# Finishing and sending batch 14's output by chunk instead of by bank, with one feature sum moved to VectorE and two steps moved ahead of a turn in batch 1's period

## The chip, the cores and the metric

The kernel runs on one core of one Trainium2 chip. The metric is the device time of one execution in microseconds; the figure for a kernel is the median of its runs. Besides the plain runs one execution was taken with a hardware profile, and every time with a place in the program comes from that one.

## The reference

The program computes a two-direction graph attention for 16 batches of 512 nodes with 512 features. The 20 first nodes of a batch are its keys and values; the adjacency carries 11 labels for each pair. Cut to what matters:

```python
row_zero = exp_v.sum(-1) == 0
q_exp = jnp.where(row_zero[..., None], 0.0, q[:, None, :])
self_feat = jnp.concatenate([exp_v, q_exp], -1) @ W_self.T + b_self
output = self_feat
for d in range(2):
    A = adj_f if d == 0 else jnp.swapaxes(adj_f, 1, 2)
    A = A[:, :, :20, :]
    aff = einsum(qh, kh) / sqrt(32)          # 16 heads of 32
    aff = where(A.sum(-1) > 0, aff, -9e15) + (A @ w_bias + b_bias)
    w = softmax(aff)
    output += einsum(w, kv, Wout[d]) + bout[d]
return exp_v + relu(output)
```

## The kernel before, in words

Everything is float32. After a set-up of some 90 us that multiplies the weights into keys and values, the main loop (`for b in range(B - 1)`, L1065) runs one period for each batch 0 to 14, and batch 15 is written out by hand behind it (L1263 to L1349). No scheduler reorders anything: each engine works through its instructions in the order of the code, and a semaphore holds an instruction until what it needs is there.

TensorE has three kinds of work in a period. `self_product` (L641, matmuls on L661) makes the features of batch b+1 in seven products of half size, where sums of operands replace an eighth product. `score_product` (L404, matmuls on L397) makes the scores of batch b in seven products in the same way, from feature blocks, key blocks and their sums. `attend` (L559, matmuls on L568) multiplies the softmax weights of batch b-1 with its values.

The scores of a batch lie in four blocks (c, l): c is the key half, l the node half. Products 1 and 6 accumulate in one PSUM tile `ps_a`. Between products its intermediate sums are read out: `taken` (L494, ScalarE) reads it after 1 and again after 7, and `lowered` (L501, VectorE, L502) reads it after 6 and again after 4. Product 7 accumulates into the same `ps_a`, so it may only start once `lowered` has read what stands there after 6. For each block follow `joined_with` (L506, VectorE), `weigh` (L515, VectorE: row maximum L522 and subtraction L523), `expo` (L525, ScalarE), `total` (L529, VectorE: row sum L531 and reciprocal L532), `normal` (L534, GpSimd multiplication L536) and `turn` (L540, VectorE transposition L544).

The operand sums are `feat_sum` n = 1 to 4 (L372; sum 1 on L377, the others on L384) and `key_sum`, on GpSimd unless an engine is given; sum 2 is made from sum 1, and sum 3 feeds score product 7. For batch b+1 `self_join` (L682, VectorE), `self_lift` (L684, VectorE, two instructions on L686) and `self_copy` (L679, ScalarE) empty the feature products; `mask_count` (L329) and `mask_sum` (L335) reduce the labels on VectorE. Loads are issued on SyncE's queue, some held until a named step is done, so that they go out in turn: `load_x` of the batch after next has its first quarter behind the lift, its second behind the label count; `load_cq` (two small loads of key biases) stands behind a turn.

Before `attend(b-1)` ScalarE seeds the four PSUM banks with the features (`seed_out`, L554, instructions on L555): banks 2 and 3 early, banks 0 and 1 late in the period, behind `expo(b, 1, 0)` and a `self_copy` on ScalarE's queue.

Output: `outt[b]` holds four chunks of 128 features by 512 nodes, and each chunk is one DMA of 128x512 float32 (262,144 bytes, `store`, L615). A PSUM bank a of `outsum` holds half the nodes (in turns of 32) of two chunks: banks 0 and 1 together make chunks 0 and 1, banks 2 and 3 make chunks 2 and 3. `finish` (L581, VectorE, L585) or `relieve` and `residual` (L590 on ScalarE, L597 on GpSimd, L600) do relu and the addition of x for one bank, hence for half of two chunks. `end` (L602) does the same for one chunk out of both banks: on VectorE with two instructions of 256 elements (L610), or on ScalarE (L612) and then GpSimd (L613). Before the change only batch 15, the last one, uses `end`; batch 14 (called `o`) goes by bank, chunks 2 and 3 being sent after the second `residual`, chunks 0 and 1 after the second `finish`.

Of the kernel before, what the change touches and what calls it, by code (L numbers as in the profile page):

```python
# [9 lines left out]
AF = mybir.ActivationFunctionType  # L10
# [8 lines left out]
def gat_kernel(  # L19
# [20 lines left out]
    nc = tc.nc  # L40
    B, F, N = xT.shape
# [10 lines left out]
    R = P // HL  # L52
# [11 lines left out]
    ps_s = ctx.enter_context(tc.tile_pool(name="ps_s", bufs=2, space=PSUM))  # L64
# [28 lines left out]
    sums, parts, done, cleared = {}, {}, {}, []  # L93
# [3 lines left out]
    def behind(one, other):  # L97

        if other is not None:
            info = mybir.DependencyInfo(mybir.DependencyClass.Sync, mybir.DependencyReason.DATA)  # L100
            tc.add_manual_dep(one.ins, other.ins.name, info, reason="loads in turn")
# [23 lines left out]
    def load_cq(b, ins=None):  # L125
        cqs[b] = load.tile([P, 2, HL, S], F32, tag="cq", name=f"cq{b}")
        for p in range(2):
            behind(nc.sync.dma_start(
                cqs[b][bass.ts(p, P // 2)].rearrange("p c h m -> p (c h m)"),
                cq_d[b : b + 1, bass.ts(p, H // 2)].rearrange("b h d m -> b (h d m)").partition_broadcast(P // 2),  # L130
            ), ins if p == 0 else None)
# [197 lines left out]
    def mask_count(b, h):  # L329
        a = adjs[b, h]  # L330
        cond = msk.tile([P, 2 * S], F32, tag="cond", name=f"cond{b}_{h}")
        done["count"] = nc.vector.tensor_reduce(cond, a.rearrange("p t (m l) -> p (t m) l", l=L), AX.X, ALU.add)  # L332
        nc.gpsimd.tensor_scalar(prods[b, h][:, :, L], cond, 0.0, NEG, ALU.is_le, ALU.mult)  # L333
# [20 lines left out]
    def feat_block(b, f, l):  # L354
        return sfs[b][:, 2 * f : 2 * f + 2, bass.ts(l, N // 2)]
# [16 lines left out]
    def feat_sum(b, n, engine=nc.gpsimd):  # L372

        if n < 4:
            fsums[b, n] = xsum.tile([P, 2, N // 2], F32, tag=f"f{n}", name=f"f{b}_{n}")
        if n == 1:
            engine.tensor_add(fsums[b, 1], feat_block(b, 0, 1), feat_block(b, 1, 1))  # L377
            return
        to, one, two = {
            2: lambda: (fsums[b, 2], fsums[b, 1], feat_block(b, 0, 0)),  # L380
            3: lambda: (fsums[b, 3], feat_block(b, 0, 0), feat_block(b, 0, 1)),
            4: lambda: (fsums[b, 2], feat_block(b, 1, 0), fsums[b, 2]),
        }[n]()
        done["fsum"] = engine.tensor_sub(to, one, two)  # L384

    def pair(name, n):
        return ps_s.tile([P, HL, N // 2], F32, tag=f"s{n % 2}", name=name, bufs=1)
# [141 lines left out]
    def total(b, c, l):  # L529
        sm = smalls[b, c, l] = soft.tile([P, per], F32, tag="sm", name=f"sm{b}_{c}{l}")  # L530
        nc.vector.tensor_reduce(sm, heads(weighs[b, c, l]), AX.X, ALU.add)  # L531
        done["sum"] = nc.vector.reciprocal(sm, sm)  # L532

    def normal(b, c, l):  # L534
        f = heads(weighs[b, c, l])
        done["normal"] = nc.gpsimd.tensor_mul(  # L536
            f, f, smalls.pop((b, c, l)).unsqueeze(2).to_broadcast([P, per, NG])
        )

    def turn(b, c, l):  # L540

        if b not in wts:
            wts[b] = work.tile([P, 2, 2, W], F32, tag="wt", name=f"wt{b}")
        done["turn"] = nc.vector.transpose(wts[b][:, c, l], weighs.pop((b, c, l)).rearrange("p g w -> p (g w)"))  # L544

    def new_outs(b, homes=None):
        homes = homes or ((accs, "f0"), (accs, "f1"), (accs, "c"))
        tiles = [
            pool.tile([P, 1 + (tag[0] != "f"), 512], F32, tag=tag, name=f"ps_o{b}_{tag}", bufs=1) for pool, tag in homes
        ]  # L550
        outsum.setdefault(b, []).extend(t[:, u] for t in tiles for u in range(t.shape[1]))
        return tiles
# [24 lines left out]
    def spread_out(t, a):  # L577

        return t[:, a // 2 * 2 : a // 2 * 2 + 2].rearrange("p c (n u r) -> p c u n r", u=2, r=R)[:, :, a % 2]

    def finish(b, a):  # L581

        if b not in outt:
            outt[b] = work.tile([P, C, N], F32, tag="o", name=f"o{b}", bufs=1)
        done["out", a] = nc.vector.scalar_tensor_tensor(  # L585
            spread_out(outt[b], a), outsum[b][a].rearrange("p (c n r) -> p c n r", c=2, r=R), 0.0,
            spread_out(xs[b], a), ALU.max, ALU.add,
        )

    def relieve(b, a):  # L590

        if b not in outt:
            outt[b] = work.tile([P, C, N], F32, tag="o", name=f"o{b}", bufs=1)
        to = spread_out(outt[b], a)
        nc.scalar.activation(to, outsum[b][a].rearrange("p (c n r) -> p c n r", c=2, r=R), AF.Relu)

    def residual(b, a):  # L597

        to = spread_out(outt[b], a)
        nc.gpsimd.tensor_add(to, to, spread_out(xs[b], a))  # L600

    def end(b, p, c, engine, us=slice(0, 2)):  # L602

        to, of = (
            t[:, 2 * p + c].rearrange("p (n u r) -> p u n r", u=2, r=R)[:, us] for t in (outt[b], xs[b])
        )
        ps = ends[p][:, us, bass.ts(c, N // 2)].rearrange("p u (n r) -> p u n r", r=R)
        if engine is nc.vector:
            for u in range(2):
                nc.vector.scalar_tensor_tensor(to[:, u], ps[:, u], 0.0, of[:, u], ALU.max, ALU.add)  # L610
        else:
            nc.scalar.activation(to, ps, AF.Relu)  # L612
            engine.tensor_add(to, to, of)  # L613

    def store(b, cs, ins=None):  # L615
        for c in cs:
            behind(nc.sync.dma_start(out[b, bass.ts(c, P)], outt[b][:, c]), ins)
# [63 lines left out]
    def self_join(b, f, l):  # L681
        done["joined"] = nc.vector.tensor_add(block(b, f, l), feed(b, 1), block(b, f, l))  # L682
# [10 lines left out]
    with tc.tile_pool(name="setup", bufs=1) as sp, tc.tile_pool(name="ps_acc", bufs=4, space=PSUM) as acc["pool"]:  # L693
# [18 lines left out]
        with tc.tile_pool(name="setup_k", bufs=1) as sk:  # L712
# [77 lines left out]
            ps = ps_s.tile([P, 2, 512], F32, tag="s1", name="ps_q", bufs=1)  # L790
# [11 lines left out]
            for fc in range(C):  # L802
                qp = sk.tile([P, B, NG], F32, tag="qp", name=f"qp{fc}", bufs=4)
                engine = nc.gpsimd if fc else nc.vector
# [49 lines left out]
        with tc.tile_pool(name="setup_g", bufs=3) as sg:  # L854
# [138 lines left out]
            for n, runs in enumerate(bursts):  # L993
# [14 lines left out]
                if rest:  # L1008
                    for kind in "mm" if n else ():
                        f, args = steps[kind].pop(0)  # L1010
# [3 lines left out]
                for kind in plan[n - first] if n - first < len(plan) else ():  # L1014
                    f, args = steps[kind].pop(0)
# [38 lines left out]
    accs = ctx.enter_context(tc.tile_pool(name="ps_loop", bufs=1, space=PSUM))  # L1054
# [5 lines left out]
    with tc.manual_schedule():  # L1060
# [4 lines left out]
        for b in range(B - 1):  # L1065
            one, two, more, further = b > 0, b > 1, b + 1 < B, b + 2 < B

            def at(yes, f, *args):
                if yes:
                    f(*args)  # L1070
# [8 lines left out]
                    load_xn(2, 1)  # L1079
            if b == 1:  # L1080
                self_join(1, 0, 1)
                feat_sum(1, 1)
                feat_sum(1, 2)
                total(0, 1, 0)
                normal(0, 1, 0)
                turn(0, 1, 1)
# [59 lines left out]
                spill(1)  # L1146
            lowered(b, 1, 0)
            at(more, load_keys, b + 1, range(3, 4), done["lowered"])
            at(one, turn, b - 1, 0, 1)
            at(one and more, load_cq, b + 1, done.get("turn"))  # L1150
            if more:
                self_product(b + 1, 6)
                self_lift(b + 1)
                at(further, load_x, b + 2, range(1), done["lift"])
                mask_count(b + 1, 0)
            at(further, load_x, b + 2, range(1, 2), done["count"])
            turn(b, 0, 0)
            at(further, load_x, b + 2, range(2, 3), done["turn"])
# [104 lines left out]
        b = B - 1  # L1263
        o = b - 1
# [15 lines left out]
        weigh_plain(b, 0, 0)  # L1280
        turn(o, 0, 1)
        seed_block(b, 0, 1, [pair("ps_l", 1)])
        new_outs(o, ((accs, "c"),))
        outt[o] = load.tile([P, C, N], F32, tag="x0", name=f"o{o}", bufs=1)
        seed_out(o, 0)
        seed_out(o, 1)
# [6 lines left out]
        store(b - 2, range(2, 4))  # L1293
        plain_scores(b, 0, 1)
        weigh_plain(b, 1, 0)
        new_outs(o, ((ps_s, "s0"),))
        seed_out(o, 2)
        seed_out(o, 3)
        seed_block(b, 1, 1, [accs.tile([P, 2, N // 2], F32, tag=f"f{i}", name=f"ps_e{i}") for i in range(2)])
# [3 lines left out]
        normal(b, 1, 0)  # L1303
        plain_scores(b, 1, 1, range(2))
        weigh_plain(b, 0, 1)
        ends = new_outs(b, ((ps_s, "s1"),))
        turn(b, 1, 0)
        for q in (3, 2):
            relieve(o, q)
        seed_out(b, 0)  # L1310
        seed_out(b, 1)
        total(b, 0, 1)
        normal(b, 0, 1)
        residual(o, 3)
        finish(o, 0)
        ends += new_outs(b, ((ps_s, "s0"),))
        seed_out(b, 3)
        plain_scores(b, 1, 1, range(2, 4))
        weigh_plain(b, 1, 1, 0)
# [1 line left out]
        turn(b, 0, 1)  # L1321
        total_part(b, 1, 1, 0)
        normal_part(b, 1, 1, 0, nc.gpsimd)
        residual(o, 2)
        store(o, range(2, 4))
        weigh_plain(b, 1, 1, 1)
        turn_part(b, 1, 1, 0)
        attend(b, ((0, 0, 2), (1, 0, 1)))
        total_part(b, 1, 1, 1)
        normal_part(b, 1, 1, 1, nc.vector)  # L1330
        turn_part(b, 1, 1, 1)
        finish(o, 1)
        store(o, range(2))
        spare = const.tile([P, C, WD], F32, tag="g", name=f"o{b}", bufs=1).rearrange("p c w -> p (c w)")
        outt[b] = spare[:, : C * N].rearrange("p (c n) -> p c n", c=C)

        def send(queue, c):
            queue.dma_start(out[b, bass.ts(c, P)], outt[b][:, c])

        end(b, 1, 0, nc.gpsimd)  # L1340
        send(nc.sync, 2)
        end(b, 0, 0, nc.gpsimd, slice(1, 2))
        attend(b, ((1, 1, 2),))
        end(b, 0, 0, nc.gpsimd, slice(0, 1))
        end(b, 1, 1, nc.vector)
        send(nc.sync, 3)
        end(b, 0, 1, nc.vector)
# [48 lines left out]
```

## Time and profile before

| | |
|---|---|
| median of 3 runs | 551.27 us (551.25 to 552.41) |
| the profiled execution, its own time | 551.43 us |
| its span, first to last instruction | 549.7 us |
| granted TensorE clock, mean | 0.997 |
| TensorE busy | 539.7 us (98% of the span) |
| VectorE busy | 480.2 us (87%) |
| ScalarE, GpSimd busy | 404.2 us (74%), 435.8 us (79%) |

The span is 1.7 us shorter than the execution's own time. A timeline row gives the start in us from the span's start, how long the row lasts, the engine and line, the output and inputs by the program's names with their shapes, how many instructions the row merges, and in brackets how long the engine stood idle just before and what ended that. PE is a matmul, PEld a weight load on the same engine, SPq the issue of a DMA by SyncE's queue. A row of the windows view gives the stretch, its length, the busy time of each engine, the granted clock, the share of the DMA engines and GB/s.

### The profile page before, as it was taken

The page shows a single profiled execution, that of the slowest core. Times are in us where ns is not written, and L with a number is a line of the kernel's source. Part 1 is how long each engine was busy: PE and PEld are TensorE (multiplying, and loading weights), DVE is VectorE, ACT ScalarE, POOL GpSimd, SP SyncE. Part 2 cuts the span into 40 slices and gives each one's busy share as a digit, 9 for nine tenths or more (in the row PEclk, how much of TensorE's full clock was granted, in tenths as well). Part 3 has the DMA queues.
Part 4 walks back from the last instruction along what each step waited for, and adds up shares of the span by engine and source line. Part 5 has one row for each costly group of instructions (what it writes and reads, how often), then busy time and mean ns, then how long its engine had stood idle before and what let it go on. Part 6 is the DMA issues. An engine that isn't in the chain of part 4 may idle for free.

```text
span 549.7 us, 19621 instructions
## 1 busy us (share of the span) xinstructions
PE 539.7 (98%) x7908; PEld 423.6 (77%) x7908; DVE 480.2 (87%) x708; ACT 404.2 (74%) x999; POOL 435.8 (79%) x420
## 2 busy tenths in 40 slices
PE   9999999999999999999999999999999999999994
PEld 6544368889788878787888878888878787888783
DVE  1776678888999999999999999999999999999995
ACT  1225436797897979888888888888878787877662
POOL 2637896779979797979798888888888979797565
PEclk9999999999999999999999999999999999999998
DMA  8999999978786878778776858676777677735034
GB/s 299 376 394 369 306 372 339 316 211 261 210 255 190 230 222 226 222 221 236 211 223 191 242 178 231 197 235 186 233 201 221 205 219 197 216 117 172 2 117 154
DMA packets 100530, 126.45 MB, mean 230 GB/s; under 512 B 19592, under 2 KB 68678, under 8 KB 98392
## 3 DMA queue, kind: packets, MB, share of 16 engines
q1 hardware_dynamic: 98696, 121.93, 71.1%
q0 software_dynamic: 1168, 2.23, 1.7%
q8 instruction: 62, 1.02, 0.8%
q10 hardware_dynamic: 576, 1.05, 0.5%
q14 instruction: 28, 0.23, 0.1%
HBM read 86.23 MB, written 40.24 MB: 230 GB/s over the span
## 4 chain that ended last, share of the span: by engine, by line
PE 91%; DVE 3%; DMA 3%; POOL 1%; ACT 1%; issue 1%; SPq 0%; DVEq 0%; POOLq 0%
PE ps_f L661 31%; PE ps_a L397 23%; PE ps_c L397 11%; PE ps_d L397 6%; PE ps_o_f L568 5%; PE ps_k L829 3%; PE ps_v L887 2%; PE ps_o_c L568 2%; DMA ws_q<-in_wsT 1%; PE ps_a L284 1%; DMA g_d<-st 1%; PE ps_l L397 1%; PE ps_c L284 1%; PE ps_e L397 0%; PE ps_d L284 0%
## 5 line engine op out<-in xcount | busy, mean ns | idle before, releaser
L327 ACT ACTIVATE prod<-adj,wb_sb 128x80 f32<-128x80 int32 x330 | 116.0, 430 | 0.0
L536 POOL TENSOR_TENSOR w<-w,sm 128x640 f32<-128x640 f32 x63 | 80.2, 1274 | 33.4 <-DVE sm L532 32.3
L661 PE MATMUL ps_f<-t,ws_s 128*64 128x246 f32 x720 | 80.0, 370 | 0.0
L661 PEld LDWEIGHTS ps_f<-t,ws_s 128*64 128x64 f32 x720 | 51.7, 136 | 18.9
L527 ACT ACTIVATE w<-w 128x640 f32<-128x640 f32 x60 | 43.8, 730 | 18.6 <-DVE w L523 18.6
L544 DVE STREAM_TRANSPOSE wt<-w 128x640 f32<-128x640 f32 x63 | 52.5, 834 | 1.3 <-POOL w L536 1.2
L661 PE MATMUL ps_f<-x,ws_v 128*64 128x246 f32 x480 | 52.4, 371 | 0.0
L531 DVE TENSOR_REDUCE sm<-w 128x32 f32<-128x640 f32 x63 | 51.1, 811 | 1.1 <-ACT w L527 0.9
L522 DVE TENSOR_REDUCE ps_d<-w 128x32 f32<-128x640 f32 x59 | 48.7, 826 | 1.8 <-ACT ps_d L431 0.2
L523 DVE TENSOR_TENSOR w<-w,ps_d 128x640 f32<-128x640 f32 x59 | 48.4, 821 | 2.0
L661 PEld LDWEIGHTS ps_f<-x,ws_v 128*64 128x64 f32 x480 | 34.7, 137 | 13.0
L370 POOL TENSOR_TENSOR k<-g,k 128x608 f32<-128x608 f32 x30 | 44.7, 1490 | 0.0
L397 PEld LDWEIGHTS ps_a<-g,sf 128*64 128x64 f32 x544 | 34.2, 137 | 5.9 <-issue 5.8
L397 PE MATMUL ps_a<-g,sf 128*64 128x152 f32 x544 | 38.6, 295 | 0.0
L338 DVE TENSOR_REDUCE add<-prod 128x80 f32<-128x960 f32 x32 | 36.7, 1148 | 1.7 <-POOL prod L333 1.7
L397 PE MATMUL ps_d<-g,sf 128*64 128x152 f32 x544 | 37.9, 293 | 0.0
L346 ACT COPY both<-add 64x80 f32<-64x80 f32 x128 | 32.6, 254 | 5.7 <-DVE add L338 4.6
L568 PE MATMUL ps_o_c<-wt,vd 32*32 32x256 f32 (+1 forms) x720 | 36.8, 386 | 0.0
L676 POOL TENSOR_TENSOR t<-x,t 128x492 f32<-128x492 f32 x30 | 34.9, 1163 | 1.2
L397 PEld LDWEIGHTS ps_d<-g,sf 128*64 128x64 f32 x544 | 35.3, 137 | 0.2 <-ACT sf L679 0.2
L333 POOL TENSOR_SCALAR prod<-cond 128x80 f32<-128x80 f32 x32 | 18.0, 563 | 21.6 <-DVE cond L332 20.2
L568 PE MATMUL ps_o_f<-wt,vd 32*32 32x256 f32 (+1 forms) x672 | 34.8, 386 | 0.3 <-ACT ps_o_f L555 0.3
(296 smaller groups left out, 1433.8 us busy)
## 6 DMA issues: line engine op xcount, KB each, us to landing
g<-g_d SPq DMA_DIRECT2D x60, 304.0 KB
g_d<-st SPq DMA_DIRECT2D x16, 1064.0 KB
out_T<-o SPq DMA_DIRECT2D x63, 256.0 KB
x<-in_xT SPq DMA_DIRECT2D x56, 256.0 KB
xn<-in_xn SPq DMA_DIRECT2D x48, 256.0 KB
adj<-in_adj SPq DMA_DIRECT2D x52, 220.0 KB
vd<-bd_d SPq DMA_DIRECT2D x64, 64.0 KB
nz<-nz_d SPq DMA_DIRECT2D x14, 256.0 KB
```

The costliest lines, as they stand in the source:

```text
L327: nc.scalar.activation(p[:, :, l], a[:, :, l], AF.Identity, scale=wb_sb[:, l : l + 1])
L338: done["masks"] = nc.vector.tensor_reduce(add, prods.pop((b, h)), AX.X, ALU.add)
L370: done["ksum"] = engine.tensor_sub(to, one, two)
L397: nc.tensor.matmul(slot(g)[bass.ts(p, P // 2), : HL * S].rearrange("p (h m) -> p h m", m=NG)[:, :, 1:], of(k)[:, bass.ds(first + g * P // ...
L522: nc.vector.tensor_reduce(mx, f, AX.X, ALU.max)
L523: done["weigh"] = (engine or nc.vector).tensor_sub(f, f, mx.unsqueeze(2).to_broadcast([P, per, NG]))
L527: done["exp"] = nc.scalar.activation(t, t, AF.Exp)
L531: nc.vector.tensor_reduce(sm, heads(weighs[b, c, l]), AX.X, ALU.add)
L536: done["normal"] = nc.gpsimd.tensor_mul(f, f, smalls.pop((b, c, l)).unsqueeze(2).to_broadcast([P, per, NG]))
L544: done["turn"] = nc.vector.transpose(wts[b][:, c, l], weighs.pop((b, c, l)).rearrange("p g w -> p (g w)"))
L568: nc.tensor.matmul(outsum[b][a][bass.ds(at // 2 * DH, n * DH), bass.ds(c * N // 2 + lo * P, (hi - lo) * P)].rearrange("p (n r) -> p n r", ...
L661: nc.tensor.matmul(parts[b][n in (2, 3, 5)][bass.ts(a, P // 2), bass.ts(i, HN)], lhs, x[:, k], start=False, stop=k == 1, skip_group_check= ...
```

## The change

In batch 1's period, `feat_sum(1, 1)` goes from GpSimd to VectorE, at the same place of the code, between `self_join(1, 0, 1)` and `total(0, 1, 0)`. In the same period `turn(0, 0, 1)` and the `load_cq` that waits for it go from ahead of `self_lift` and `mask_count` to behind them. Periods of other batches keep their order.

For batch 14, `end` replaces `relieve`, `residual` and `finish`. `end` now takes the tiles of the batch that it is called for, and on ScalarE and on GpSimd it is a call for each, so that the ScalarE part can stand earlier than the GpSimd part. Chunks 0 and 2 are sent in the middle of batch 15's work, chunk 3 where chunks 2 and 3 were sent, chunk 1 where 0 and 1 were. Batch 15 keeps its instructions (`both` calls ScalarE and then GpSimd).

```diff
-                feat_sum(1, 1)
+                feat_sum(1, 1, nc.vector)
...
-            at(one, turn, b - 1, 0, 1)
-            at(one and more, load_cq, b + 1, done.get("turn"))
+            at(two, turn, b - 1, 0, 1)
+            at(two and more, load_cq, b + 1, done.get("turn"))
             if more:
                 self_product(b + 1, 6)
                 self_lift(b + 1)
                 at(further, load_x, b + 2, range(1), done["lift"])
                 mask_count(b + 1, 0)
+            if b == 1:
+                turn(0, 0, 1)
+                load_cq(2, done["turn"])
...
-        for q in (3, 2):
-            relieve(o, q)
+        for c in range(2):
+            end(o, 1, c, nc.scalar)
...
-        residual(o, 3)
-        finish(o, 0)
+        end(o, 1, 0, nc.gpsimd)
+        end(o, 0, 0, nc.vector)
+        store(o, (0, 2))
...
-        residual(o, 2)
-        store(o, range(2, 4))
+        end(o, 1, 1, nc.gpsimd)
+        store(o, (3,))
...
-        finish(o, 1)
-        store(o, range(2))
+        end(o, 0, 1, nc.vector)
+        store(o, (1,))
```

VectorE at the start of batch 1's period, before (`sf_1191` are batch 1's features, `w_10_1245` and `w_11_1283` weight blocks of batch 0, `w_00_1478` the first block of batch 1):

```order
L682 TENSOR_TENSOR sf_1191<-ps_f_1_1147,sf_1191 128x2x246
L531 TENSOR_REDUCE sm_10_1465<-w_10_1245 128x32
L532 RECIPROCAL sm_10_1465<-sm_10_1465 128x32
L544 STREAM_TRANSPOSE wt_1264<-w_11_1283 128x640
L508 TENSOR_TENSOR w_00_1478<-ps_d_1409,w_00_1478 128x640
```

And there in the change (whose lines stand one number higher from L613 on):

```order
L683 TENSOR_TENSOR sf_1191<-ps_f_1_1147,sf_1191 128x2x246
L377 TENSOR_TENSOR f_1_1461<-sf_1191 128x512
L531 TENSOR_REDUCE sm_10_1465<-w_10_1245 128x32
L532 RECIPROCAL sm_10_1465<-sm_10_1465 128x32
L544 STREAM_TRANSPOSE wt_1264<-w_11_1283 128x640
L508 TENSOR_TENSOR w_00_1478<-ps_d_1409,w_00_1478 128x640
```

One instruction, feature sum 1, stands ahead of all that VectorE does next, and GpSimd's queue begins that stretch with feature sum 2.

VectorE in the middle of batch 1's period, before (`w_01_1405` is batch 0's last block, `sf_1528` are batch 2's features):

```order
L502 TENSOR_TENSOR w_10_1585<-ps_a_1407,both_0_1289 128x640
L544 STREAM_TRANSPOSE wt_1264<-w_01_1405 128x640
L686 SCALAR_TENSOR_TENSOR sf_1528<-nz_1382,qwD,ps_f_0_1472 128x246 x2
L332 TENSOR_REDUCE cond_0_1604<-adj_0_1384 128x80
L544 STREAM_TRANSPOSE wt_1608<-w_00_1478 128x640
```

And there in the change:

```order
L502 TENSOR_TENSOR w_10_1585<-ps_a_1407,both_0_1289 128x640
L687 SCALAR_TENSOR_TENSOR sf_1528<-nz_1382,qwD,ps_f_0_1472 128x246 x2
L332 TENSOR_REDUCE cond_0_1600<-adj_0_1384 128x80
L544 STREAM_TRANSPOSE wt_1264<-w_01_1405 128x640
L544 STREAM_TRANSPOSE wt_1608<-w_00_1478 128x640
```

The turn of batch 0's last block stands behind the lift and the label count, next to the turn of batch 1's first block.

SyncE's queue at that place, before (`x` are batch 3's quarters, `cq` the key biases of batch 2):

```order
L139 DMA g_1458<-g_d 128x4x152
L128 DMA cq_1589<-cq_d 64x320 x2
L111 DMA x_1602<-in_xT 128x512 x4
L117 DMA xn_0_1666<-in_xn 128x512
L206 DMA nz_d<-nz_3_1640 128x4
```

And there in the change:

```order
L139 DMA g_1458<-g_d 128x4x152
L111 DMA x_1598<-in_xT 128x512
L128 DMA cq_1604<-cq_d 64x320 x2
L111 DMA x_1598<-in_xT 128x512 x3
L117 DMA xn_0_1666<-in_xn 128x512
```

The first quarter of batch 3's x goes out ahead of the two bias loads, the rest behind them.

More of the change, by code (lines that the diff above doesn't have):

```diff
@@ L606, in end @@
         )
-        ps = ends[p][:, us, bass.ts(c, N // 2)].rearrange("p u (n r) -> p u n r", r=R)
+        ps = ends[b][p][:, us, bass.ts(c, N // 2)].rearrange("p u (n r) -> p u n r", r=R)
         if engine is nc.vector:
@@ L610, in end @@
                 nc.vector.scalar_tensor_tensor(to[:, u], ps[:, u], 0.0, of[:, u], ALU.max, ALU.add)
+        elif engine is nc.scalar:
+            nc.scalar.activation(to, ps, AF.Relu)
         else:
-            nc.scalar.activation(to, ps, AF.Relu)
             engine.tensor_add(to, to, of)
@@ L1282, in gat_kernel @@
         seed_block(b, 0, 1, [pair("ps_l", 1)])
-        new_outs(o, ((accs, "c"),))
+        ends = {o: new_outs(o, ((accs, "c"),))}
         outt[o] = load.tile([P, C, N], F32, tag="x0", name=f"o{o}", bufs=1)
@@ L1295, in gat_kernel @@
         weigh_plain(b, 1, 0)
-        new_outs(o, ((ps_s, "s0"),))
+        ends[o] += new_outs(o, ((ps_s, "s0"),))
         seed_out(o, 2)
@@ L1305, in gat_kernel @@
         weigh_plain(b, 0, 1)
-        ends = new_outs(b, ((ps_s, "s1"),))
+        ends[b] = new_outs(b, ((ps_s, "s1"),))
         turn(b, 1, 0)
-        for q in (3, 2):
-            relieve(o, q)
+        for c in range(2):
+            end(o, 1, c, nc.scalar)
         seed_out(b, 0)
@@ L1313, in gat_kernel @@
         normal(b, 0, 1)
-        residual(o, 3)
-        finish(o, 0)
-        ends += new_outs(b, ((ps_s, "s0"),))
+        end(o, 1, 0, nc.gpsimd)
+        end(o, 0, 0, nc.vector)
+        store(o, (0, 2))
+        ends[b] += new_outs(b, ((ps_s, "s0"),))
         seed_out(b, 3)
@@ L1338, in send, with both @@
             queue.dma_start(out[b, bass.ts(c, P)], outt[b][:, c])
-        end(b, 1, 0, nc.gpsimd)
+        def both(*args):
+            end(b, *args[:2], nc.scalar, *args[2:])
+            end(b, *args[:2], nc.gpsimd, *args[2:])
+        both(1, 0)
         send(nc.sync, 2)
-        end(b, 0, 0, nc.gpsimd, slice(1, 2))
+        both(0, 0, slice(1, 2))
         attend(b, ((1, 1, 2),))
-        end(b, 0, 0, nc.gpsimd, slice(0, 1))
+        both(0, 0, slice(0, 1))
         end(b, 1, 1, nc.vector)
```

## The prediction

> **What bounds the kernel now.** I read the page first, then TensorE's waits over the whole run, then timelines of the two places that the change touches: batch 1's period and the end.
>
> The page's first line gives the span. In the waits of TensorE's matmuls one row alone lies in the main loop:
>
> ```profile
> span 549.7 us, 19621 instructions
> ```
>
> ```profile
> PE ps_o_f L568 <- ACT ps_o_f L555: 0.3, 1, 0.3
> ```
>
> So in 15 periods TensorE is held almost nowhere, and an edit that only takes busy time off another engine is worth nothing unless it ends a wait of TensorE. The one wait is for the output seeds ahead of `attend`. The timeline of TensorE in batch 1's period, then the same steps in batch 2's:
>
> ```profile
> 141.36 2.26 PE L397 MATMUL ps_a<-k,sf 128*64 128x152 f32 x32
> 143.96 0.92 PE L568 MATMUL ps_o_f<-wt,vd 32*32 32x256 f32 x3 [0.34 <-ACT ps_o_f L555]
> ...
> 146.88 0.87 PE L397 MATMUL ps_a<-g,sf 128*64 128x152 f32 x10
> ```
>
> ```profile
> 170.97 2.24 PE L397 MATMUL ps_a<-k,sf 128*64 128x152 f32 x32
> ...
> 175.53 0.74 PE L397 MATMUL ps_a<-g,sf 128*64 128x152 f32 x8
> ```
>
> From score product 4 to the next batch's product 1 it is 146.88 - 141.36 = 5.52 us in period 1 and 175.53 - 170.97 = 4.56 us in period 2. The difference, 0.96 us, is what late seeds cost in period 1. ScalarE's timeline says why:
>
> ```profile
> 142.07 0.74 ACT L527 ACTIVATE w<-w 128x640 f32<-128x640 f32 x1 [0.42 <-DVE w L523]
> ...
> 143.31 1.12 ACT L555 ACTIVATE ps_o_f<-sf 128x512 f32<-128x512 f32 x2
> ```
>
> The seeds end at 144.43, 0.8 us after product 4's 143.62. Ahead of them on the queue stands an `expo` that waited for VectorE's subtraction: VectorE is late in this period, and VectorE in turn waited twice for GpSimd:
>
> ```profile
> 129.55 0.84 DVE L544 STREAM_TRANSPOSE wt<-w 128x640 f32<-128x640 f32 x1 [1.21 <-POOL w L536]
> ...
> 134.42 0.83 DVE L508 TENSOR_TENSOR w<-ps_c,w 128x640 f32<-128x640 f32 x1 [0.48 <-POOL w L499]
> ```
>
> At the end of the program the DMA engines are the bound: this is costed below.
>
> **Feature sum 1 on VectorE: what it costs.** VectorE, GpSimd and TensorE around it:
>
> ```profile
> 119.06 0.66 DVE L682 TENSOR_TENSOR sf<-ps_f,sf 128x492 f32<-128x492 f32 x1
> 119.64 0.81 DVE L531 TENSOR_REDUCE sm<-w 128x32 f32<-128x640 f32 x1
> ...
> 120.75 0.79 DVE L544 STREAM_TRANSPOSE wt<-w 128x640 f32<-128x640 f32 x1
> 121.64 0.82 DVE L508 TENSOR_TENSOR w<-ps_d,w 128x640 f32<-128x640 f32 x1
> ```
>
> ```profile
> 119.24 2.29 PE L397 MATMUL ps_d<-g,sf 128*64 128x152 f32 x32
> ```
>
> ```profile
> 119.87 1.28 POOL L377 TENSOR_TENSOR f<-sf 128x512 f32<-128x512 f32 x1 [2.01 <-DVE sf L682]
> 121.22 1.28 POOL L384 TENSOR_TENSOR f<-f,sf 128x512 f32<-128x512 f32 x1
> ```
>
> ```profile
> 541.21 0.49 DVE L478 TENSOR_TENSOR w<-w,sm 128x320 f32<-128x320 f32 x1
> ```
>
> No row of before shows this sum on VectorE with GpSimd idle. The nearest two are the multiplication of 320 elements out of SBUF in 0.49 us and the addition of 640 in 0.82; between them 512 elements give 0.69 us, and I take that (bounds 0.5 and 0.82; a third row, far away, is a rival below). It starts when L682 ends, 119.72, so it ends at 120.41, and the row sum starts some 0.08 earlier than that, as it now does against L682: 120.33 for 119.64, a shift of 0.69. A little of it is swallowed at once: the L508 at 121.64 began 0.10 after the transposition's end (121.54), where the row sum began 0.08 ahead of L682's end; it had waited for TensorE's `ps_d` (121.53). That is 0.18 of slack, so about 0.5 to 0.55 us of shift stays, and I take 0.55.
>
> From there to `lowered` VectorE has no gap, and that matters, for TensorE waits behind it:
>
> ```profile
> 127.58 0.76 DVE L502 TENSOR_TENSOR w<-ps_a,both 128x640 f32<-128x640 f32 x1
> ```
>
> ```profile
> 128.48 2.29 PE L397 MATMUL ps_a<-g,f 128*64 128x152 f32 x32
> ```
>
> ```profile
> 128.45 2.04 PEld L397 LDWEIGHTS ps_a<-g,f 128*64 128x64 f32 x32 [0.31 <-POOL f L384]
> ```
>
> ```profile
> 127.01 1.28 POOL L384 TENSOR_TENSOR f<-sf 128x512 f32<-128x512 f32 x1
> ```
>
> Score product 7 needs feature sum 3 (GpSimd, done 128.29) and `lowered`'s read of `ps_a` (done 128.34); TensorE began 0.16 after the former. With the shift `lowered` ends at 128.34 + 0.55 = 128.89, and product 7 starts 0.16 later, at 129.05 instead of 128.48. So the change puts a new wait of **+0.57 us** on TensorE, 13 us ahead of the one that it aims at. Everything that TensorE does behind it comes 0.57 later.
>
> **What it and the moved turn gain.** GpSimd is rid of 1.28 us: sum 2 starts at 120.41 + 0.15 (the distance from L682's end to 119.87) = 120.56, not 121.22, and GpSimd goes on 0.66 us earlier. VectorE no longer stands 1.21 us ahead of the turn, since lift and label count (whose inputs are there) fill the gap. What is late next is the block that VectorE joins at 134.42:
>
> ```profile
> 130.81 0.71 ACT L495 ACTIVATE w<-ps_a 128x640 f32<-128x640 f32 x1
> ```
>
> ```profile
> 132.83 1.56 POOL L499 TENSOR_TENSOR w<-w,both 128x640 f32<-128x640 f32 x1
> ```
>
> Its read-out on ScalarE follows product 7, now 129.05 + 2.29 = 131.34, and ends near 132.1; GpSimd's L499 then runs from 132.2 to 133.75, not 132.83 to 134.39. VectorE's join there comes 0.6 earlier, VectorE has no gap from it to the subtraction that `expo` waits for, and so the seeds end near 143.85 instead of 144.43. TensorE now gets to `attend` at 143.62 + 0.57 = 144.19. The seeds are 0.3 us ahead: the 0.96 goes entirely. Net for this half: 0.57 - 0.96 = **-0.39 us**.
>
> The bias loads wait about 1 us longer in SyncE's queue, with three x quarters and the loads of xn behind them; batch 2 reads the biases on ScalarE some 12 us later and x in the next period, so I cost that at nothing (their cover gone, it would show as a TensorE wait after 144). Does VectorE carry a debt into period 2? Its next read of `ps_a` waits for product 4, which ends 0.57 later, so VectorE gains next to nothing there while TensorE gains 0.39. In period 2 VectorE has this much idle time:
>
> ```profile
> 151.35 0.82 DVE L508 TENSOR_TENSOR w<-ps_d,w 128x640 f32<-128x640 f32 x1 [0.43 <-PE ps_d L397]
> ```
>
> That covers it, and later periods are ordered as before, so -0.39 is passed to the end.
>
> **Output by chunk.** VectorE, the issue queue and the DMA engines at the end:
>
> ```profile
> 535.57 0.63 DVE L585 SCALAR_TENSOR_TENSOR o<-ps_o_c,x 128x512 f32<-128x512 f32 x1
> 536.56 0.49 DVE L463 TENSOR_REDUCE mx<-ps_e 128x16 f32<-128x320 f32 x1 [0.37 <-PE ps_e L397]
> ...
> 542.16 0.65 DVE L585 SCALAR_TENSOR_TENSOR o<-ps_o_c,x 128x512 f32<-128x512 f32 x1
> 543.49 1.42 DVE L610 SCALAR_TENSOR_TENSOR o<-ps_o_s,x 128x256 f32<-128x256 f32 x4 [0.68 <-issue]
> ```
>
> ```profile
> 542.85 0.81 SPq L617 DMA_DIRECT2D out_T<-o  x2
> ```
>
> ```profile
> 543.75 1.52 SPq L1338 DMA_DIRECT2D out_T<-o  x3
> ```
>
> ```profile
> 543.50:544.00 0.50, 0.00 (x0) 0.00 (x0) 0.50 (x2) 0.26 (x1) 0.34 (x2) 1.00 0.63 233
> 544.00:547.50 3.50, 0.00 (x0) 0.00 (x0) 0.91 (x3) 0.00 (x0) 0.56 (x1) 0.87 1.01 382
> 547.50:548.00 0.50, 0.00 (x0) 0.00 (x0) 0.00 (x0) 0.00 (x0) 0.00 (x0) 0.50 0.62 238
> ```
>
> In the last stretch the DMA engines are full at 382 GB/s. The first half microsecond moves 0.117 MB, so the flow starts near 543.69; the last moves 0.119 MB, so it ends at 547.81. That is 1.57 MB, six chunks of 262,144 bytes at 0.686 us each: chunks 0 and 1 of batch 14 (issued from 542.85, 0.84 us ahead of the flow) and the four of batch 15. Now chunk 0 goes out near 536.4, chunk 2 near 538.4, and one chunk less stands in this queue. The pair of VectorE instructions lasts (1.42 - 0.42) / 3 + 0.42 = 0.75 instead of 0.65, so chunk 1 is issued 0.10 later, its flow starts at 543.79, and five chunks end at 543.79 + 3.43 = 547.22. Batch 15's last chunk is issued by 545.27, so its data are ready before its turn. Gain 547.81 - 547.22 = **-0.59 us**. The longer pairs lie in the idle 0.37 and 0.68 behind them; GpSimd and ScalarE keep count, size and place of their instructions.
>
> Sum: -0.39 - 0.59 = -0.98 us. The profiled execution took 551.43, 1.7 more than its span and 0.16 more than the median; I expect 550.45 of it, and of the median 551.27 - 0.98 = 550.3.
>
> **Rivals.** *No new wait at product 7.* If `lowered` does not hold TensorE (no wait of before shows it doing so, the row names feature sum 3), the half in batch 1 gives the whole -0.96: -1.55, 549.7. For it: TensorE went on within 0.16 of either. Against it: both write and read `ps_a`, and the read ended last.
>
> *Nothing in batch 1.* If VectorE's 0.55 is not won back by the join at 134.42 (GpSimd late there through something else), seeds come at 144.43 as before, TensorE trades one wait for the other, and only the output gains: -0.59, 550.7. The 1.21 that VectorE saves speaks against it.
>
> *Slower: the sum meets GpSimd.* The set-up's end shows the same sum on VectorE, and what GpSimd began just before:
>
> ```profile
> 91.71 2.98 DVE L377 TENSOR_TENSOR f<-sf 128x512 f32<-128x512 f32 x1
> ```
>
> ```profile
> 91.63 1.49 POOL L370 TENSOR_TENSOR k<-g,k 128x608 f32<-128x608 f32 x1
> ```
>
> At 2.98 in place of 0.69, product 7 waits 0.57 + 2.29 = 2.86; less 0.96 and 0.59 that is +1.31, 552.6. It turns into a loss from a duration of 0.69 + 0.98 = 1.67. It needs GpSimd at work when the sum starts, and the 2.01 us that GpSimd idles ahead of 119.87 speak against it; its next instruction needs this very sum. The Trainium skill has this as a rule (SBUF — State Buffer, "Who interferes with whom"): a VectorE instruction with two SBUF inputs contends with a GpSimd instruction that reads SBUF, and whichever starts first keeps the other out for the whole instruction. The 2.98 agrees with that rule; by it the sum here costs 2.98 only if GpSimd is first.
>
> **How the numbers follow.** Forecast 0.62, no new wait 0.15, nothing in batch 1 0.17, slower 0.06. The forecast's own range, from the sum's 0.5 to 0.82 and 0.15 either way on the output, is 550.0 to 550.7. With the two neighbours, and 0.2 either way for the spread of a median (the two lower runs of before lie 0.02 apart, the third 1.1 above), the range is 549.5 to 551.3, which leaves out the slow case and little else. A measurement of this kernel tells about 0.2% (1.1 us) from no change, so faster means under 550.17: all of the second case and a third of the first, 0.37. Slower is 0.06, the same 0.57.
>
> **What would show it.** Product 7 of batch 1 starts near 129.05 and its wait is put down to VectorE; `attend` follows product 4 without a wait, and the next batch begins near 146.5; all later periods lie 0.4 earlier; the last full stretch of the DMA engines is 0.7 shorter. I am wrong in the first half if L377 on VectorE lasts over 1 us or product 7 is on time, and in the second if the last chunk lands as late as before against VectorE's last instruction.

## The result

The changed kernel takes 550.71 us (median of 22 runs, 550.07 to 551.36); the kernel before, in the same set of runs, 551.58 us (22 runs). The ratio is 0.9984, interval [0.9977, 0.999]: 0.87 us less, or 0.16%, which is real and still inside the 0.2% that the prediction called no change. The forecast was -0.98 us.

The profiled execution took 550.91 us, its span is 549.1 us at a granted clock of 0.997. One thing must be taken out before its rows are laid beside those of before: batch 1's product 1 starts at 117.50 us here and at 117.05 there. That is set-up, of which the change edits nothing (more on it at the end); so 0.45 us is subtracted in the loop. First, the waits of TensorE's matmuls over the whole run, after:

```profile
span 549.1 us, 19626 instructions
```

```profile
PE ps_a L397 <- DVE w L502: 0.5, 1, 0.5
```

The wait for the output seeds (0.3) is gone from this list, and a wait for `lowered` stands there that before did not have. TensorE's timeline after shows both places:

```profile
117.50 2.24 PE L397 MATMUL ps_a<-g,sf 128*64 128x152 f32 x32
...
129.52 2.29 PE L397 MATMUL ps_a<-g,f 128*64 128x152 f32 x32 [0.49 <-DVE w L502]
...
142.40 2.27 PE L397 MATMUL ps_a<-k,sf 128*64 128x152 f32 x32
...
146.99 2.29 PE L397 MATMUL ps_a<-g,sf 128*64 128x152 f32 x32
```

Product 7 starts at 129.52 - 0.45 = 129.07, where before had 128.48. From product 4 to the next product 1 it is 4.59 us, where before had 5.52. VectorE's timeline after, from the moved sum to the join that ends the chain:

```profile
119.51 0.66 DVE L683 TENSOR_TENSOR sf<-ps_f,sf 128x492 f32<-128x492 f32 x1
120.28 0.69 DVE L377 TENSOR_TENSOR f<-sf 128x512 f32<-128x512 f32 x1
120.89 0.81 DVE L531 TENSOR_REDUCE sm<-w 128x32 f32<-128x640 f32 x1
...
122.72 0.79 DVE L508 TENSOR_TENSOR w<-ps_d,w 128x640 f32<-128x640 f32 x1
...
128.61 0.76 DVE L502 TENSOR_TENSOR w<-ps_a,both 128x640 f32<-128x640 f32 x1
129.29 0.84 DVE L687 SCALAR_TENSOR_TENSOR sf<-nz,qwD,ps_f 128x246 f32<-128x246 f32 x2
130.05 1.06 DVE L332 TENSOR_REDUCE cond<-adj 128x80 f32<-128x880 int32 x1
131.03 1.62 DVE L544 STREAM_TRANSPOSE wt<-w 128x640 f32<-128x640 f32 x2
...
134.22 0.82 DVE L508 TENSOR_TENSOR w<-ps_c,w 128x640 f32<-128x640 f32 x1 [0.54 <-POOL w L499]
```

The sum lasts 0.69 us. Behind `lowered` VectorE has no gap up to the two transpositions, so the 1.21 us of waiting is gone. The join waits still, for GpSimd; GpSimd's and ScalarE's rows say for what:

```profile
121.05 1.28 POOL L384 TENSOR_TENSOR f<-f,sf 128x512 f32<-128x512 f32 x1 [2.77 <-DVE f L377]
...
131.85 0.56 POOL L333 TENSOR_SCALAR prod<-cond 128x80 f32<-128x80 f32 x1
132.63 1.55 POOL L499 TENSOR_TENSOR w<-w,both 128x640 f32<-128x640 f32 x1 [0.22 <-ACT w L495]
```

```profile
131.85 0.71 ACT L495 ACTIVATE w<-ps_a 128x640 f32<-128x640 f32 x1 [0.62 <-PE ps_a L397]
...
143.13 1.12 ACT L555 ACTIVATE ps_o_f<-sf 128x512 f32<-128x512 f32 x2
```

GpSimd waits 0.22 us for ScalarE's read-out, and that waits for product 7: the chain into the seeds now starts on TensorE itself. The seeds end at 143.13 + 1.12 = 144.25, less 0.45 that is 143.80.

The end of the program after, by windows (length, busy time of PE, PEld, VectorE, ScalarE and GpSimd, then clock, DMA share, GB/s):

```profile
543.50:544.00 0.50, 0.00 (x0) 0.00 (x0) 0.40 (x2) 0.36 (x1) 0.35 (x2) 1.00 0.27 106
544.00:547.00 3.00, 0.00 (x0) 0.00 (x0) 1.02 (x4) 0.00 (x0) 0.66 (x1) 0.81 1.00 380
547.00:547.50 0.50, 0.00 (x0) 0.00 (x0) 0.00 (x0) 0.00 (x0) 0.00 (x0) 0.50 0.62 238
547.50:548.00 0.50, 0.00 (x0) 0.00 (x0) 0.00 (x0) 0.00 (x0) 0.00 (x0) 0.50 0.00 0
```

These hold 0.053 + 1.14 + 0.119 = 1.31 MB, five chunks of 262,144 bytes. By the packet records the flow ends 2.42 us after VectorE's last instruction, and 3.05 us before the change.

So the trace gives -0.35 us in batch 1's period and -0.63 us at the end, -0.98 together, plus 0.45 us of set-up: -0.53, and the two spans (549.13 and 549.65 us before rounding) differ by 0.52.

### The profile page after: what moved, and what is told of

The parts are those of the page before. It is cut to its first block, busy times and chain, and to the rows that moved or that the text cites. A ratio compares the mean times of both kernels' runs of the same rounds, so it can differ in the third digit from the quotient of the medians.

```text
span 549.1 us, 19626 instructions
## 1 busy us (share of the span) xinstructions
PE 540.0 (98%) x7908; PEld 423.6 (77%) x7908; DVE 481.1 (88%) x711; ACT 404.3 (74%) x999; POOL 434.4 (79%) x419
## 4 chain that ended last, share of the span: by engine, by line
PE 93%; DVE 4%; issue 1%; ACT 1%; POOL 0%; DVEq 0%; ACTq 0%; POOLq 0%
PE ps_f L662 30%; PE ps_a L397 23%; PE ps_c L397 11%; PE ps_d L397 6%; PE ps_o_f L568 5%; PE ps_v L888 3%; PE ps_k L830 3%; PE ps_o_c L568 2%; PE ps_kv L772 1%; PE ps_a L284 1%; PE ps_l L397 1%; PE ps_c L284 1%; PE ps_warm L732 1%; DVE sm L531 1%; DVE ps_d L522 0%
## 5 line engine op out<-in xcount | busy, mean ns | idle before, releaser
L199 ACT ACTIVATE xn<-xn 128x512 f32<-128x512 f32 x56 | 34.5, 620 | 0.0
```

## The experiments

Each kernel computes the whole of the reference. Beside the times, four lengths from each profile are compared, so that set-up drops out: batch 1's period (from the start of its product 1 to the start of batch 2's), product 7's start after product 1's, the stretch from product 4 to the next product 1, and the end of the last DMA flow after VectorE's last instruction. They are worked out from unrounded starts, in us.

| kernel | ratio to before, interval | period 1 | to product 7 | product 4 to next | flow's end |
|---|---|---|---|---|---|
| before | | 29.83 | 11.43 | 5.52 | 3.05 |
| the change | 0.9984 [0.9977, 0.999] | 29.48 | 12.02 | 4.59 | 2.42 |
| batch 1's half alone | 0.9993 [0.9984, 1.0002] | 29.49 | 12.02 | 4.59 | 3.05 |
| output half alone | 0.9991 [0.9982, 1.0] | 29.84 | 11.44 | 5.53 | 2.42 |
| sum alone, first profile | 0.9992 [0.9984, 1.0001] | 29.95 | 12.49 | 4.59 | 3.06 |
| sum alone, again | 0.9996 [0.9988, 1.0005] | 29.48 | 12.01 | 4.59 | 3.05 |
| turn alone | 0.9996 [0.9987, 1.0005] | 29.65 | 11.44 | 5.34 | 3.06 |
| read of `ps_a` first | 0.998 [0.997, 0.9989] | 29.04 | 11.33 | 4.85 | 2.42 |
| sum made twice | 1.0002 [0.9994, 1.0011] | 30.21 | 12.74 | 4.59 | 2.43 |
| GpSimd kept busy | 1.0 [0.9991, 1.0008] | 30.48 | 13.02 | 4.59 | 2.42 |
| chunk 0 behind 3 | 0.9978 [0.997, 0.9987] | 29.48 | 12.02 | 4.59 | 2.42 |
| chunk 0 behind 1 | 0.9994 [0.9986, 1.0003] | 29.48 | 12.02 | 4.59 | 3.08 |
| count late | 0.9965 [0.9953, 0.9977] | 29.01 | 11.33 | 4.83 | 2.42 |
| count behind the join | 0.9972 [0.9961, 0.9983] | 28.78 | 11.33 | 4.59 | 2.43 |

Period 2 is 28.65 us in all of them, but for 28.68 in the last; from VectorE's last instruction back to batch 14's product 1 it is 54.27 or 54.28 us in all.

### The two halves apart

Batch 1's half is the change with the output code of before; the output half is the reverse:

```diff
-                feat_sum(1, 1, nc.vector)
+                feat_sum(1, 1)
...
-            at(two, turn, b - 1, 0, 1)
+            at(one, turn, b - 1, 0, 1)
...
-            if b == 1:
-                turn(0, 0, 1)
```

> Batch 1's period as in the change, the output as before. Theory (the sum puts a new wait of about 0.5 us on score product 7 and, with the moved turn, takes away the 0.96 us at attend): from the start of batch 1's score product 1 to the start of batch 2's the profile of before shows 146.88 - 117.05 = 29.83 us; here 29.5, and the whole time is 0.35 us below before. Rival (the gain is all in the output, the two waits of the period cancel): 29.8 and no change.

> The output by chunk as in the change, batch 1's period as before. Theory: the period stays at 29.83 us, the last full flow of the DMA engines holds five chunks and ends 0.6 us sooner after VectorE's last instruction than in before (there 547.81 - 544.91 = 2.9 us), and the whole time is 0.6 us below before. Rival (all the gain is here): 0.9 us below before.

The first shortens period 1 by 0.34 us and leaves the flow's end; the second shortens the flow by 0.63 us and leaves the period. Together they are the change's 0.35 and 0.63. The medians (-0.41 and -0.59 us against 551.57) agree, though neither interval excludes no change: it is the lengths in the traces that put the rival "nothing in batch 1" out.

### Where the new wait comes from

The change with the read of `ps_a` ahead of the row sum in batch 1:

```diff
-            total(b, 0, 0)
-            at(more, load_keys, b + 1, range(2, 3), done["sum"])
-            normal(b, 0, 0)
+            if b != 1:
+                total(b, 0, 0)
+                at(more, load_keys, b + 1, range(2, 3), done["sum"])
+                normal(b, 0, 0)
...
             lowered(b, 1, 0)
+            if b == 1:
+                total(1, 0, 0)
+                load_keys(2, range(2, 3), done["sum"])
+                normal(1, 0, 0)
```

> The change, and in batch 1's period lowered(1, 0) ahead of total(0, 0) on VectorE in place of behind it. Theory (lowered, late by the sum, is what holds score product 7): lowered ends 1.1 us earlier, product 7 starts without a wait, the period takes 29.83 - 0.96 - 0.1 = 28.8 to 28.9 us, and the whole time is 0.5 to 0.65 us below the change, 1.4 to 1.6 below before. Rival (product 7 is held by something else, or the seeds become late again): the period stays near 29.5 and the time at the change's.

And the change with the sum made twice:

```diff
                 feat_sum(1, 1, nc.vector)
+                feat_sum(1, 1, nc.vector)
```

> The change, with feature sum 1 of batch 1 made twice on VectorE, one behind the other. Theory: VectorE has no slack between the sum and lowered, so product 7 starts 0.6 us later still and the seeds stay ahead of attend; the period takes 30.1 us and the whole time is 0.6 us above the change. Rival (VectorE has slack there, and the wait at product 7 has another cause): period and time as in the change.

With the read first, TensorE's list has no wait for `lowered`, and product 7 starts 11.33 us after product 1. Of the 0.69 us so freed, 0.45 reaches the period. That is less than was expected (29.04 us, not 28.8 to 28.9), and the rival was right in part: from product 4 to the next product 1 it is 4.85 us, so the seeds are late again, by 0.26. TensorE's and ScalarE's timelines of this kernel:

```profile
128.86 2.26 PE L397 MATMUL ps_a<-g,f 128*64 128x152 f32 x32
...
143.90 0.66 PE L568 MATMUL ps_o_f<-wt,vd 32*32 32x256 f32 x3
```

```profile
142.99 1.12 ACT L555 ACTIVATE ps_o_f<-sf 128x512 f32<-128x512 f32 x2
```

`attend` begins at 143.90 and the last seed ends at 144.11. With the sum made twice, the two take 1.42 us in one row, and product 7's wait grows from 0.49 to 1.21 us; the period grows by 0.72, nearly the whole of the second sum. So the wait at product 7 is VectorE's work ahead of `lowered`. That is shown from both sides: 0.72 us more of it costs TensorE 0.72, and without the wait product 7 comes 0.69 us earlier.

### The sum and the turn apart

The sum without the moved turn, the moved turn without the sum (both with the output code of before), each the part of the change's diff that names it.

> Only feature sum 1 of batch 1 on VectorE; turn and output as before. Theory (what frees VectorE later is GpSimd's queue being 0.66 us ahead; the turn's move adds nothing to it): period 29.5 us as with both edits, 0.35 us below before. Rival (the moved turn makes the gain, the sum only costs): product 7 waits 0.5 us and attend still waits, the period takes 29.8 us or more.

> Only the turn and the bias loads of batch 1's period behind lift and label count; sum and output as before. Theory: no wait at product 7 by VectorE; the label column on GpSimd comes some 0.25 us earlier (it stood idle 0.25 for the count), so the join at 134.42 comes 0.27 earlier and the seeds too; the period takes 29.55 us, 0.27 below before. Rival (the turn alone makes the gain): the wait at attend goes, 28.9 us, 0.9 below before.

The first profile of the sum alone gave 29.95 us, against the expectation. Product 7 was 0.47 later than in the change, and ScalarE's timeline shows an input that was late:

```profile
120.73 0.97 ACT L622 ACTIVATE ps_f<-nz,qw 128x246 f32<-128x246 f32 x2 [1.78 <-DMA nz<-nz_d]
```

Batch 2's flags landed 1.78 us after ScalarE was ready for them. SyncE issues that load once the store that writes the flags is done. SyncE waited 4.2 us for the store here and 2.2 to 3.4 us in the other profiles. Of those only "count late" shows ScalarE waiting for the flags, for 0.50 us, which did not reach product 7 (11.33 us, as with the read first alone). So the same kernel was profiled again:

> The same kernel as the sum alone, once more. Its first profile had ScalarE wait 1.78 us for the load of batch 2's flags ahead of the first feed, which no other profile shows. Theory (an accident of that load in one execution): with the flags in time product 7 starts 12.02 us after product 1, batch 1's period is 29.48 to 29.50 us and attend follows without a wait. Rival (without the moved turn the sum costs more): product 7 at 12.4 us or later and a period of 29.9 us again, with no wait for the flags.

The same row with the flags in time:

```profile
118.86 0.97 ACT L622 ACTIVATE ps_f<-nz,qw 128x246 f32<-128x246 f32 x2
```

The period is then 29.48 us, the same as with both edits: beside the moved sum the moved turn is worth nothing. VectorE's 1.21 us of waiting is gone although the turn stands where it stood, as VectorE's and GpSimd's timelines of this second profile show:

```profile
127.96 0.76 DVE L502 TENSOR_TENSOR w<-ps_a,both 128x640 f32<-128x640 f32 x1
128.71 0.85 DVE L544 STREAM_TRANSPOSE wt<-w 128x640 f32<-128x640 f32 x1
```

```profile
127.39 1.28 POOL L536 TENSOR_TENSOR w<-w,sm 128x640 f32<-128x640 f32 x1
...
131.99 1.55 POOL L499 TENSOR_TENSOR w<-w,both 128x640 f32<-128x640 f32 x1
```

Counted from product 1 (116.86 here, 117.05 before), `lowered` ends 0.57 us later than before, and the multiplication that the turn needs ends 0.65 us earlier: together 1.22, against the 1.21 of waiting. L499 starts 15.13 us after product 1, in the change too.

Alone the turn is worth 0.18 us (29.65) where 0.27 was expected, and its seeds are late still; TensorE's and GpSimd's timelines of the turn alone:

```profile
143.74 0.92 PE L568 MATMUL ps_o_f<-wt,vd 32*32 32x256 f32 x3 [0.16 <-ACT ps_o_f L555]
```

```profile
130.63 1.26 POOL L536 TENSOR_TENSOR w<-w,sm 128x640 f32<-128x640 f32 x1
131.98 0.56 POOL L333 TENSOR_SCALAR prod<-cond 128x80 f32<-128x80 f32 x1
132.62 1.55 POOL L499 TENSOR_TENSOR w<-w,both 128x640 f32<-128x640 f32 x1
```

GpSimd has no idle time of note here (under 0.1 us between these rows): with feature sum 1 still in its queue, L499 comes as the queue lets it. In the change, with the sum gone, it waits for product 7's read-out in place of its queue. The two edits go after one wait, and the sum suffices.

### The sum against a busy GpSimd

The change, with three equal key sums on GpSimd in place of one, so that it is at work when feature sum 1 starts:

```diff
             key_sum(b, 2)
...
+                key_sum(1, 2)
+                key_sum(1, 2)
```

> The change, with key sum 2 of batch 1 made three times on GpSimd, so that GpSimd is at work (to about 120.7) when VectorE's feature sum 1 starts (119.75). It computes the same values. Theory (the sum meets GpSimd's reads, as the 2.98 us row in the set-up's end): the sum takes 1.6 to 1.8 us in place of 0.69, product 7 waits 1 us more, the whole time is 1 us above the change, level with before. Rival (no contention for this sum): the sum stays at 0.69 us, only GpSimd is 0.3 us later, and the time is within 0.1 us of the change.

GpSimd's and VectorE's timelines of this kernel:

```profile
117.50 4.60 POOL L370 TENSOR_TENSOR k<-g,k 128x608 f32<-128x608 f32 x3
```

```profile
120.95 1.70 DVE L377 TENSOR_TENSOR f<-sf 128x512 f32<-128x512 f32 x1
```

```profile
131.20 2.29 PE L397 MATMUL ps_a<-g,f 128*64 128x152 f32 x32 [1.49 <-DVE w L502]
```

The sum takes 1.70 us, 1.01 over the 0.69, and ends 0.55 us after GpSimd's last key sum (122.10). Product 7's wait takes up all of it, and the period is 1.00 longer. The slower rival's mechanism is real; its condition is absent in the change, where GpSimd idles for 2.77 us until the sum is there.

Its price of 2.98 us was too high. The set-up of before has more rows behind the two that the prediction shows, on GpSimd and then on VectorE:

```profile
93.08 1.04 POOL L676 TENSOR_TENSOR t<-x 128x492 f32<-128x492 f32 x1
94.21 1.48 POOL L676 TENSOR_TENSOR t<-x,t 128x492 f32<-128x492 f32 x1
```

```profile
94.72 1.51 DVE L384 TENSOR_TENSOR f<-f,sf 128x512 f32<-128x512 f32 x1
```

The sum there ended at 94.69, 0.56 us after GpSimd's second instruction (94.13 from unrounded times), so it outlasted two of them. The addition behind it ended 0.55 us after the third (95.68). In batch 1 GpSimd's next instruction needs the sum itself, so only one can hold it up, and this kernel comes out level with before (ratio 1.0), where the prediction's price gave 1.31 us more.

### The output's last flow

The change with chunk 0 of batch 14 issued later, first behind chunk 3, then behind chunk 1:

```diff
-        store(o, (0, 2))
+        store(o, (2,))
...
-        store(o, (1,))
+        store(o, (0, 1))
```

> The change, but chunk 0 of batch 14 is sent at the end, ahead of chunk 1, in place of near 536.4. Theory (the end is one flow of the DMA engines, 0.69 us for each chunk in it): six chunks again, the end 0.6 to 0.7 us later than in the change against VectorE's last instruction, the whole time 0.3 us below before. Rival (the gain came from the finishing of the chunks, not from when they are sent): as the change.

This missed its expectation, because it did not test what it was meant to. Chunk 0's data had long been ready, so SyncE issued it right behind chunk 3, at 541.26 us, ahead of its wait for chunk 1; the last flow still held five chunks, and time and lengths are those of the change. It shows only that chunk 0 may as well go out then. The second try has `store(o, (1, 0))`:

> The changed kernel, but chunk 0 of batch 14 is issued right behind chunk 1, so that it stands in the last queue again. Theory (the gain at the end is one chunk less in the last full stretch of the DMA engines): six chunks in that stretch, the last of them down 3.05 to 3.1 us after VectorE's last instruction (2.42 in the change), so about 0.65 us over the change, and 0.2 to 0.4 us under before. Rival (the gain is in the way the chunks are finished, not in their number in the last stretch): 2.42 us as in the change, and its time. Batch 1's period 29.48 us by both.

Its windows at the end:

```profile
543.50:544.00 0.50, 0.00 (x0) 0.00 (x0) 0.50 (x3) 0.00 (x0) 0.46 (x1) 1.00 1.02 385
544.00:547.00 3.00, 0.00 (x0) 0.00 (x0) 0.61 (x2) 0.00 (x0) 0.26 (x1) 0.57 1.02 380
547.00:547.50 0.50, 0.00 (x0) 0.00 (x0) 0.00 (x0) 0.00 (x0) 0.00 (x0) 0.50 1.00 393
547.50:548.00 0.50, 0.00 (x0) 0.00 (x0) 0.00 (x0) 0.00 (x0) 0.00 (x0) 0.50 0.15 53
```

These hold 1.56 MB, near six chunks (1.57), and the flow's end is back at 3.08 us although the chunks are finished as in the change. The gain at the end is the one chunk fewer in that flow, and nothing else of the edit.

### What is late behind product 7

On top of the read of `ps_a` first, the second label count on VectorE is moved behind the subtraction ahead of the last `expo`:

```diff
-                mask_count(b + 1, 1)
+                if b != 1:
+                    mask_count(b + 1, 1)
...
             weigh(b, 1, 0)
+            if b == 1:
+                mask_count(2, 1)
```

> The changed kernel with the read of ps_a ahead of the row sum in batch 1 (product 7 without its wait, which left seeds 0.26 us late at attend), and the second label count of batch 1's period on VectorE moved behind the subtraction that the next expo waits for. Theory (the seeds are late by VectorE's queue): the subtraction ends 0.6 to 0.95 us earlier, the seeds are in time, from product 4 to the next product 1 4.59 us in place of 4.85, batch 1's period 28.78 us (29.04 without the move, 29.48 in the change); 0.7 us under the change, about 1.6 under before. Rival (GpSimd, which gets the count late, or the mask's end becomes the wait): a period of 29.04 us or more, with a new wait of TensorE behind product 4 or in the next period.

This fell short of the expected 4.59: from product 4 to the next product 1 it is still 4.83 us, though the `expo` came 0.39 us earlier after product 1 than with the read first alone. ScalarE's timeline of this kernel names what was left:

```profile
141.05 0.74 ACT L527 ACTIVATE w<-w 128x640 f32<-128x640 f32 x1
...
143.17 0.60 ACT L555 ACTIVATE ps_o_f<-sf 128x512 f32<-128x512 f32 x1 [0.28 <-DVE sf L683]
```

The last seed waits for VectorE's join of batch 2's features, which empties the PSUM bank that the seed takes over, and the count now stood ahead of that join. So it goes one step further back:

```diff
                         self_join(b + 1, 0, 1)
+                        if b == 1:
+                            mask_count(2, 1)
```

> As the run with the late count, but the count stands on VectorE one step further back, behind the join of batch 2's self products whose bank the last output seed takes over. Open after that run: its subtraction ended 0.6 us earlier, and yet 4.83 us from product 4 to the next product 1 remained, where 4.59 is no wait; its last seed waited 0.28 us for that join. Theory (the last seed is late by the join behind the count): the seeds end near 143.3 us on that clock, attend has no wait, 4.59 us and a period of batch 1 of 28.78 us; 0.25 us under the run with the late count, about 1.85 under before. Rival (something else holds attend, or GpSimd, whose count and feature sum 1 come about 1 us later, is waited for in batch 2's period): 4.83 us again, or a period 2 longer than 28.65.

ScalarE's and TensorE's timelines of it:

```profile
142.14 1.12 ACT L555 ACTIVATE ps_o_f<-sf 128x512 f32<-128x512 f32 x2
```

```profile
117.08 2.24 PE L397 MATMUL ps_a<-g,sf 128*64 128x152 f32 x32
...
141.26 2.27 PE L397 MATMUL ps_a<-k,sf 128*64 128x152 f32 x32
145.85 2.29 PE L397 MATMUL ps_a<-g,sf 128*64 128x152 f32 x32
```

The last seed now ends at 143.26 and the stretch is 4.59 us: TensorE waits there no longer. The period is 28.78 us against 29.48 in the change and 29.83 before; period 2 is 0.03 longer. Both kernels with the count moved are faster than before, by 0.35% and 0.28% (549.85 us, 5 runs, and 550.17 us, 7 runs, against 551.67 and 551.66); the second's interval reaches down to 0.17%. Their two intervals overlap; the times do not tell which of them is ahead. The traces say the second, by 0.23 us in period 1 less 0.03 in period 2.

## Why the prediction was right

- **The sum on VectorE, 0.69 us.** Measured 0.69. But it starts 0.11 us after the end that it was to follow (119.83 against 119.72), so the row sum behind it is 0.80 us late, not 0.69. The 0.18 of slack came off as costed: the shift was 0.63 us at the next join (122.72 - 0.45 against 121.64) and 0.58 at `lowered`. The prediction took 0.55 where its own 0.69 - 0.18 gives 0.51; that this met the 0.58 is partly luck.
- **The new wait, +0.57 at product 7.** Measured 129.07 where 129.05 stood, put down to VectorE. Reading `ps_a` earlier removes it, a second sum adds 0.72 us to it; the rival without a new wait is out.
- **The late seeds, -0.96.** The stretch shrank by 0.93 us; the seeds end at 143.80, where 143.85 was forecast, and the net is -0.35 for the -0.39.
- **What the moved turn gains.** This step is right in its sum and wrong in how it shares it out. The prediction set VectorE's 1.21 us against the rival of no gain in batch 1, as though the moved turn were needed. The sum alone brings all, the turn alone 0.18. With the sum alone VectorE's 1.21 is gone too, because GpSimd is 0.65 us ahead (0.66 was costed) and VectorE 0.57 behind.
- **Passed on to the end.** Period 2 is 28.65 us before and after, so no debt was carried.
- **The output, -0.59.** Measured -0.63. The pair of VectorE instructions was costed at 0.75 us; the two pairs last 0.69 and 0.72, and the flow starts 0.06 later against VectorE's last instruction, where 0.10 was taken.
- **The time.** The median before was 551.58 us in these runs, not 551.27; less 0.98 that is 550.6, and 550.71 was measured. The interval (-1.27 to -0.55 us) would also hold the -0.59 of the rival "nothing in batch 1": the time alone does not confirm the mechanism, the lengths do.

## What to carry to other kernels

An instruction given to a second engine costs its length, less the slack on the way, where the bounding engine next waits on that engine: look for the first read that it needs, which may stand far ahead of the wait that the edit is for. Two edits that go after the same wait do not add, and when a wait goes, the next thing late must be named before its whole length is counted. At the end of a program count the bytes in the last full stretch of the DMA engines; what is sent before that stretch begins comes off the time.

## What was not expected of the chip

- The loop repeats far more closely than the time does. Period 0 and periods 2 to 13 agree within 0.04 us between all the kernels, while batch 1's product 1, always 26.15 us after batch 0's, starts anywhere between 116.65 and 118.18 us. That spread of the set-up, whose code none of them edits, is larger than the whole effect, so lengths between two rows of one trace settled what the times alone could not. In the nine profiles with the new output code it starts at 117.08 or later, in the five without at 117.05 or earlier. If the output edit lengthened the set-up, the medians with it would lie above what the lengths add up to. On the whole they do not: medians and lengths agree within 0.18 us for all kernels, with the output edit and without (the sum alone taken by its second profile), but for "count late" (0.37 us faster than its lengths, 5 runs).
- A load that must wait for the store of its source came too late in two of the fourteen profiles, by 1.78 and 0.50 us, with the same code at that place; the first cost 0.47 us in that trace, the second nothing at product 7. One profile of such a kernel can give a false reading.
- An addition on VectorE that began during GpSimd's key sum took 1.70 us in place of 0.69, and ended 0.55 us after that key sum did. In the set-up two more ended 0.56 and 0.55 us after a GpSimd instruction, one of them after two instructions in a row.
